# Adding two lanes of the bias network's last layer by DMA, so that TensorE closes four steps at a time instead of two

## The chip, the cores and the metric

The kernel runs on one core of one Trainium2 chip, in f32 throughout. The metric is device time in microseconds (us) of one launch, the median of several runs; lower is better.

## The reference

Two layers follow each other on x of shape (2, 512, 32, 32). The first is a deformable attention block with eight groups of 64 channels, the second a plain single-head attention over the 1024 pixels with 512 channels. Nearly all that matters here is one part of the first layer: a small network gives a bias for each pair of a pixel (1024 of them) and a sampled key (64 of them), for each of the 16 combinations of batch and group.

```python
pos  = grid_q[:, :, None, :] - grid_kv[:, None, :, :]      # 16 x 1024 x 64 x 2
bias = sign(pos) * log1p(abs(pos))
bias = relu(bias @ cpb_w1 + cpb_b1)                        # 2 -> 128
bias = relu(bias @ cpb_w2 + cpb_b2)                        # 128 -> 128, the costly one
bias = (bias @ cpb_w3 + cpb_b3)                            # 128 -> 1
sim  = q . k + bias ; attn = softmax(sim) ; out = attn . v
```

Around it lie grouped 1x1 convolutions, a 6x6 depthwise convolution that gives the keys' offsets, the sampling of the keys, an output projection, a two-layer MLP with 2048 hidden channels, and the second attention.

## The kernel before, in words

**Stages.** A head of some 42 us makes the queries and the key offsets of the first two groups. Then comes the stage of the bias network, 256 steps, up to about 1988 us. Then the projection, the MLP (each product by Strassen's seven multiplications) and the second attention, up to 2742 us. The change touches the head and the stage of the bias network.

**A step.** `NS = NG * NSL` is 16 groups times 16 steps. A step `s` handles four keys against all 1024 pixels. `st_layer1(s)` on VectorE (DVE) adds two small tables and clamps at zero: a tile `h1` of 128 channels x 4096. `st_layer2(s)` on TensorE (PE) multiplies it by `cw2`, the 128x128 weights of the second layer, in four blocks `z` of 32 output channels. Each block is eight matmuls into one PSUM tile of two banks: partition 32q + l of that tile is key q and lane l, where lane l stands for the four channels that the four blocks give at that place. ScalarE (ACT) takes each block out of PSUM with the ReLU: blocks 0 and 2 as they are into `rx`, blocks 1 and 3 scaled by their weight of the third layer into `ua` and `ub`.

**The third layer.** It is a dot product over 128 channels, and most of it is done before TensorE sees it. `st_sum(s, 0)` on DVE adds weight times `rx` to `ua`, `st_sum(s, 2)` the same for `ub`. For a scaled ReLU to keep its meaning the weights of one lane must have one sign, so the head sorts out signs: `swap` on GpSimd (POOL) exchanges channels within a lane where needed, and `sc[:, 8]` keeps the sign of each lane. Then a DMA that adds (`accum_op`), issued from POOL, adds `ub` to `ua` (line L583), for all but the last `LAST = 2` steps. `st_layer3` closes two steps at a time: four matmuls of 128x512 with `w3s`, which holds the lanes' signs, sum the 32 lanes of each key into the scores `sim` of the group in PSUM (line L604). At a group's last closing the q.k matmuls go into the same tile, and `softmax_steps` follows in the background over the next steps.

**Order.** The loop over `s` writes `st_sum(s-1, 2)`, `st_layer1(s+2)`, `st_layer2(s)`, `st_sum(s, 0)`, one piece of background work (`later`: the offsets and keys of the later groups; `softmax_steps`), and at odd `s` `st_layer3(s-3)`. A scheduler orders each engine's queue, and every engine runs its queue in order. Each wait, also for a DMA's landing, is made by the queue that holds the waiting instruction. SyncE (SP) issues `load_tables` (`fb`, once in four steps), and the loads and stores of the background work.

**Buffers.** `h1` has 3, `rx` 3, `ua` 5, `ub` 4, PSUM tiles for the blocks 3, `sim` 2.

Of the kernel before, what the change touches and what calls it, by code (L numbers as in the profile page):

```python
# [14 lines left out]
P = 128  # L15
# [7 lines left out]
LAST = 2  # L23
# [14 lines left out]
    ("w1x", 1), ("w1y", 1), ("cb2", 4), ("w3", 4), ("dww", 36),  # L38
# [10 lines left out]
def conv_seq_kernel(ctx: ExitStack, tc: tile.TileContext, x, xt, kst, cst, vec, wsm, outw, w1, w2, wl, out):  # L49
# [4 lines left out]
    kp = cp.tile([P, 384], F32, name="kp")  # L54
# [3 lines left out]
    ident = kp[:, 0:128]  # L58
# [11 lines left out]
    w3s = cp.tile([P, 60], F32, name="w3s")  # L70
    nc.gpsimd.memset(w3s, 0.0)
# [22 lines left out]
    with tc.tile_pool(name="lp", bufs=2) as lp, tc.tile_pool(name="ph", bufs=1) as ph:  # L94
# [30 lines left out]
        nc.scalar.dma_start(out=kp, in_=kst)  # L125
# [19 lines left out]
        def swap(w, of, n):  # L145
            w = w.rearrange("p (z c) -> p z c", z=4)
            t = ph.tile([P, 10, n], F32, tag="hx" if n > 1 else "swap", name=f"swap{n}")
            g, ne, a1, a3, keep, t0, t1 = t[:, 0:4], t[:, 4], t[:, 5], t[:, 6], t[:, 7], t[:, 8], t[:, 9]
            nc.gpsimd.tensor_scalar(g, w, 0.0, None, ALU.is_ge)
            for o, u, v in ((ne, g[:, 1], g[:, 3]), (a1, g[:, 0], g[:, 1])):  # L150
                nc.gpsimd.tensor_tensor(o, u, v, ALU.subtract)
                nc.gpsimd.tensor_tensor(o, o, o, ALU.mult)
            nc.gpsimd.tensor_tensor(a1, a1, ne, ALU.mult)
            nc.gpsimd.tensor_tensor(a3, ne, a1, ALU.subtract)
            nc.gpsimd.tensor_scalar(keep, ne, -1.0, 1.0, ALU.mult, ALU.add)
            for dst, src in of:
                d, v = (e.rearrange("p (z c) -> p z c", z=4) for e in (dst, src))
                nc.gpsimd.tensor_copy(d[:, 2], v[:, 2])
                nc.gpsimd.tensor_tensor(d[:, 0], v[:, 0], keep, ALU.mult)
                for z, a in ((1, a1), (3, a3)):  # L160
                    nc.gpsimd.tensor_tensor(t0, v[:, z], a, ALU.mult)
                    nc.gpsimd.tensor_tensor(d[:, 0], d[:, 0], t0, ALU.add)
                    nc.gpsimd.tensor_scalar(t1, a, -1.0, 1.0, ALU.mult, ALU.add)
                    nc.gpsimd.tensor_tensor(t1, t1, v[:, z], ALU.mult)
                    nc.gpsimd.tensor_tensor(t0, v[:, 0], a, ALU.mult)
                    nc.gpsimd.tensor_tensor(d[:, z], t0, t1, ALU.add)

        swap(kp[:, 256:384], [(cw2, kp[:, 128:256])], 32)
        w3 = vs[:, VOFF["w3"] : VOFF["w3"] + 4]
        swap(w3, [(sc[:, 0:4], w3), (sc[:, 4:8], vs[:, VOFF["cb2"] : VOFF["cb2"] + 4])], 1)  # L170
        nc.gpsimd.tensor_scalar(sc[:, 8:9], sc[:, 1:2], 0.0, 2.0, ALU.is_ge, ALU.mult)
        nc.gpsimd.tensor_scalar(sc[:, 8:9], sc[:, 8:9], 1.0, None, ALU.subtract)
        nc.gpsimd.tensor_scalar(sc[:, 0:4], sc[:, 0:4], sc[:, 8:9], None, ALU.mult)
        for z in (1, 3):
            nc.gpsimd.tensor_tensor(sc[:, 4 + z : 5 + z], sc[:, 4 + z : 5 + z], sc[:, z : z + 1], ALU.mult)
        for u in range(4):
            nc.gpsimd.tensor_copy(w3s[32 * u : 32 * u + 32, 28 + u : 29 + u], sc[32 * u : 32 * u + 32, 8:9])
# [154 lines left out]
        def sample(ci):  # L332
# [23 lines left out]
            for i, (b, k) in enumerate(G):  # L356
# [29 lines left out]
                for f in range(2):  # L386
                    r = slice(64 * f, 64 * f + 64)
                    d = kvz[r, f, :].rearrange("p (e i t) -> p e i t", e=2, t=4)
                    v, u = (
                        t[r].rearrange("p (i e t) -> p e i t", e=2, t=4)  # L390
                        for t in (ps[:, 0:J], sg[:, 4, f, i * J : (i + 1) * J])
                    )
                    for e in range(2):
                        nc.vector.scalar_tensor_tensor(
                            d[:, e], v[:, e], bns[r, k : k + 1], u[:, e], ALU.mult, ALU.add
                        )
# [103 lines left out]
        for _ in head:  # L500
            pass
        next(v)
# [55 lines left out]
        def st_layer2(s):  # L558
            h1 = h1s.pop(s)
            r = []  # L560
            for z in range(4):
                ps = zp.tile([P, 2, 512], F32, name="ps2")
                for h in range(2):
                    for q in range(4):
                        nc.tensor.matmul(  # L565
                            ps[32 * q : 32 * q + 32, h, :], cw2[:, 32 * z : 32 * z + 32],
                            h1[:, 16 * h : 16 * h + 16, q, :], start=True, stop=True,
                        )
                o = lp.tile([P, 2, 512], F32, name=("rx", "ua", "rx", "ub")[z], bufs=(3, 5, 3, 4)[z])
                if z % 2 == 0:  # L570
                    nc.scalar.activation(o, ps, AF.Relu, bias=sc[:, 4 + z : 5 + z])  # L571
                else:
                    nc.scalar.activation(o, ps, AF.Relu, bias=sc[:, 4 + z : 5 + z], scale=sc[:, z : z + 1])  # L573
                r.append(o)
                if z % 2 == 1:
                    evicted.setdefault(s, []).append(nc.cur_bb.bb.instructions[-1])
            sums[s] = r

        def st_sum(s, z):
            r = [t.rearrange("p h n -> p (h n)") for t in sums[s][z : z + 2]]  # L580
            nc.vector.scalar_tensor_tensor(r[1], r[0], sc[:, z : z + 1], r[1], ALU.mult, ALU.add)  # L581
            if z == 2 and s < NS - LAST:
                nc.gpsimd.dma_start(out=sums[s][1], in_=sums[s][3], accum_op=ALU.add)  # L583

        def st_layer3(s):
            gi, i = divmod(s // 2, NSL // 2)
# [3 lines left out]
            if i == NSL // 2 - 1:  # L590
# [8 lines left out]
            parts = (1,) if s < NS - LAST else (1, 3)  # L599
            for z in parts:  # L600
                for h in range(2):
                    for e in range(2):
                        q = 64 * h + 32 * e
                        nc.tensor.matmul(  # L604
                            sims[gi][q : q + 32, :], w3s[:, 28 - 4 * i : 60 - 4 * i], sums[s + e][z][:, h, :],
                            start=(i == 0), stop=(i == NSL // 2 - 1 and z == parts[-1]),
                        )
            for e in range(2):
                sums.pop(s + e)
# [63 lines left out]
        for s in range(NS):  # L673
            if s > 0:
                st_sum(s - 1, 2)
            if s % 4 == 0 and s // 4 + 1 < 4 * NG:
# [15 lines left out]
            if s % 2 == 1 and s >= 3:  # L692
                st_layer3(s - 3)
                if (s - 2) % NSL == NSL - 1:
                    tail = softmax_steps(s // NSL - 1)
        st_sum(NS - 1, 2)
        st_layer3(NS - 2)
# [455 lines left out]

def _layout(np, inputs):
# [7 lines left out]
    def twice(v):  # L1162
# [8 lines left out]
        "cb2": np.tile(L0["cpb_b2"].reshape(4, 32).T, (4, 1)),  # L1171
        "w3": np.tile(L0["cpb_w3"].reshape(4, 32).T, (4, 1)),
# [27 lines left out]
    def quarters(w):  # L1200
# [9 lines left out]
        "kst": np.concatenate(  # L1210
            [np.eye(P, dtype=np.float32), L0["cpb_w2"], np.broadcast_to(L0["cpb_w3"].reshape(1, P), (P, P))],
            axis=1,
        ),
# [26 lines left out]
```

## Time and profile before

| | |
|---|---|
| median of 3 runs | 2741.42 us (2740.01 to 2743.95) |
| time of the profiled execution | 2744.24 us |
| its span, first to last instruction | 2742.5 us |
| granted TensorE clock | 0.998 |
| PE busy | 2721.3 us, 99% of the span |
| DVE busy | 2248.2 us, 82% |
| ACT busy | 1686.6 us, 61% |
| POOL busy | 374.7 us, 14% |
| DMA busy in most of the stage (mean of 16 engines) | four tenths |

Busy time is the union of an engine's instructions; a group's "mean ns" is that of one record, and an f32 matmul leaves two records. Matmuls overlap in the array, so that the mean duration of one is not what it costs: the distance from one start to a later one is. Idle time before a group is put down to the engine or DMA that ended it. A DMA's time "to landing" counts from the start of its issue on the queue that issues it.

### The profile page before, as it was taken

How to read it: one execution, taken by the hardware profiler on the slowest of the kernel's cores; microseconds unless marked ns; L12 is line 12 of the kernel's file. 1: busy time of each engine (PE TensorE's matmuls, PEld its weight loads, DVE VectorE, ACT ScalarE, POOL GpSimd, SP SyncE). 2: the span in 40 equal slices, each digit the busy share in tenths (PEclk: the TensorE clock that was granted, in tenths of full speed). 3: DMA queues.
4: the chain of work that ended last, by engine and by line, in shares of the span. 5: the costliest groups of instructions: out<-in, count | busy, mean ns of one | idle time of the engine just before them, and what ended most of it. 6: DMA issues, size and time to landing. Idle time of an engine off the chain costs nothing.

```text
span 2742.5 us, 46612 instructions
## 1 busy us (share of the span) xinstructions
PE 2721.3 (99%) x20114; PEld 975.2 (36%) x20114; DVE 2248.2 (82%) x1327; ACT 1686.6 (61%) x2164; POOL 374.7 (14%) x430
## 2 busy tenths in 40 slices
PE   9999999999999999999999999999999999999999
PEld 3322323233334333333333333333334444446455
DVE  6999999998999899999999999999774574466454
ACT  4786897788878788866866776686722022124040
POOL 3111111111111111111111111111162233000000
PEclk9999999999999999999999999999999999999999
DMA  5444444444444444444444444444331011000000
GB/s 186 93 95 94 91 97 86 94 99 95 86 88 98 101 85 85 95 92 86 89 95 88 85 93 89 89 93 86 70 138 43 35 46 46 16 16 0 31 0 31
DMA packets 64685, 214.32 MB, mean 78 GB/s; under 512 B 11104, under 2 KB 13664, under 8 KB 61792
## 3 DMA queue, kind: packets, MB, share of 16 engines
q0 software_dynamic: 36864, 135.28, 26.7%
q1 hardware_dynamic: 26752, 74.98, 7.7%
q8 instruction: 159, 2.61, 0.4%
q10 hardware_dynamic: 864, 1.07, 0.1%
q14 instruction: 46, 0.38, 0.0%
HBM read 71.59 MB, written 6.55 MB: 28 GB/s over the span
## 4 chain that ended last, share of the span: by engine, by line
PE 91%; DVE 4%; issue 2%; ACT 2%; DMA 1%; SPq 0%; POOL 0%; DVEq 0%; ACTq 0%; POOLq 0%
PE ps L565 58%; PE sw L850 14%; PE sw L967 9%; PE sim L604 4%; PE sw L1065 2%; DVE h L548 2%; PE sw L796 1%; PE psg L454 1%; DVE ua L581 0%; PE sim L595 0%; DVE ub L581 0%; DMA fb<-fdr 0%; PE pkv L380 0%; DMA ua<-ub 0%; ACT rx L571 0%
## 5 line engine op out<-in xcount | busy, mean ns | idle before, releaser
L565 PE MATMUL ps<-h,cw 128*32 128x512 f32 x16384 | 1790.9, 593 | 7.1 <-ACT rx L571 4.8
L548 DVE CUSTOM_DVE_ANT_1 h<-ta,tb 128x4096 f32<-128x4096 f32 (+1 forms) x257 | 1131.7, 4404 | 88.7 <-PE ps L565 85.0
L565 PEld LDWEIGHTS ps<-h,cw 128*32 128x32 f32 x16384 | 535.4, 110 | 1224.0 <-issue 1170.2
L571 ACT ACTIVATE rx<-ps,sc 128x1024 f32<-128x1024 f32 x512 | 568.7, 1111 | 219.7 <-PE ps L565 216.3
L583 POOL DMA_DIRECT2D ua<-ub x254 | 220.5, 868 | 1697.2 <-DVE ub L581 1609.4
L573 ACT ACTIVATE ua<-ps,sc 128x1024 f32<-128x1024 f32 x256 | 308.4, 1205 | 117.1 <-PE ps L565 116.7
L573 ACT ACTIVATE ub<-ps,sc 128x1024 f32<-128x1024 f32 x256 | 307.9, 1203 | 89.3 <-PE ps L565 89.0
L581 DVE SCALAR_TENSOR_TENSOR ua<-rx,sc,ua 128x1024 f32<-128x1024 f32 x256 | 327.4, 1279 | 34.8 <-ACT ua L573 34.6
L581 DVE SCALAR_TENSOR_TENSOR ub<-rx,sc,ub 128x1024 f32<-128x1024 f32 x256 | 326.7, 1276 | 5.8 <-ACT ub L573 5.6
L850 PE MATMUL sw<-xb,w1t 128*128 128x512 f32 x448 | 193.7, 592 | 1.3 <-DVE xs L730 1.3
L850 PE MATMUL sw<-hm,w2t 128*128 128x512 f32 x448 | 193.6, 592 | 0.0
L730 DVE TENSOR_TENSOR hm<-hm,sw 128x1024 f32<-128x1024 f32 x56 | 67.6, 1219 | 112.4 <-PE sw L850 112.2
L604 PE MATMUL sim<-ua,w3s 128*32 128x512 f32 x1024 | 135.5, 594 | 0.2 <-DMA ua<-ub 0.2
L850 PEld LDWEIGHTS sw<-xb,w1t 128*128 128x128 f32 x448 | 85.0, 190 | 108.8 <-issue 105.2
L850 PEld LDWEIGHTS sw<-hm,w2t 128*128 128x128 f32 x448 | 85.1, 190 | 107.1 <-issue 106.4
L859 ACT ACTIVATE hm<-hm,vs 128x512 f32<-128x512 f32 x64 | 42.7, 714 | 129.4 <-DVE hm L730 129.4
L730 DVE TENSOR_TENSOR xs<-xs,sw 128x1024 f32<-128x1024 f32 (+1 forms) x48 | 55.5, 1170 | 75.7 <-PE sw L967 36.0
L529 ACT ACTIVATE ta<-fb,vs 128x512 f32<-128x512 f32 x64 | 88.3, 1379 | 17.5 <-DMA fb<-fdr 17.5
L967 PE MATMUL sw<-aT,vt 128*128 128x512 f32 x224 | 96.7, 593 | 0.3 <-ACT aT L1047 0.3
L884 ACT COPY hm<-sw 128x1024 f32<-128x1024 f32 x8 | 8.1, 1010 | 133.6 <-PE sw L850 133.6
L714 POOL TENSOR_TENSOR w1t<-w1t 128x512 f32<-128x512 f32 x32 | 60.4, 1909 | 111.7 <-DMA w1t<-in_w 111.1
L245 ACT ACTIVATE prod<-qa,vs 128x56 f32<-128x56 f32 (+4 forms) x180 | 64.0, 440 | 0.0
(221 smaller groups left out, 1551.4 us busy)
## 6 DMA issues: line engine op xcount, KB each, us to landing
ua<-ub POOLq DMA_DIRECT2D x254, 512.0 KB, 4.7
fb<-fdr SPq DMA_DIRECT2D x64, 512.0 KB, 5.1
w1t<-in_w SPq DMA_DIRECT2D x8, 1024.0 KB, 4.9
w2t<-in_w SPq DMA_DIRECT2D x8, 1024.0 KB, 4.8
xn<-in_x SPq DMA_DIRECT2D x8, 512.0 KB, 5.2
xnt<-in_xt SPq DMA_DIRECT2D x8, 512.0 KB, 5.7
xs<-in_x SPq DMA_DIRECT2D x16, 256.0 KB, 5.9
out<-xs SPq DMA_DIRECT2D x16, 256.0 KB, 2.1
```

What stands on the lines that cost most here:

```text
L245: nc.scalar.activation(dst, src, AF.Copy, scale=col("dww", 12 * m + t))
L529: nc.scalar.activation(ta.rearrange("p j x -> p x j"), fb[:, 0], AF.Identity, bias=col("cb1"), scale=col("w1x"))
L548: nc.vector._custom_dve(TENSOR_ADD_SAT, out=h1[:, y : y + step].rearrange("p y t x -> p (y t x)"), in0=a.unsqueeze(1).to_broadcast([P, ste ...
L565: nc.tensor.matmul(ps[32 * q : 32 * q + 32, h, :], cw2[:, 32 * z : 32 * z + 32], h1[:, 16 * h : 16 * h + 16, q, :], start=True, stop=True,)
L571: nc.scalar.activation(o, ps, AF.Relu, bias=sc[:, 4 + z : 5 + z])
L573: nc.scalar.activation(o, ps, AF.Relu, bias=sc[:, 4 + z : 5 + z], scale=sc[:, z : z + 1])
L581: nc.vector.scalar_tensor_tensor(r[1], r[0], sc[:, z : z + 1], r[1], ALU.mult, ALU.add)
L583: nc.gpsimd.dma_start(out=sums[s][1], in_=sums[s][3], accum_op=ALU.add)
L604: nc.tensor.matmul(sims[gi][q : q + 32, :], w3s[:, 28 - 4 * i : 60 - 4 * i], sums[s + e][z][:, h, :], start=(i == 0), stop=(i == NSL // 2 ...
L730: nc.vector.tensor_tensor(out, a, b_, op)
L850: nc.tensor.matmul(ps[:, m, :], w[:, a, k, m * P : (m + 1) * P], x[:, b_, k, :], start=(k == 0), stop=(k == 1),)
L967: nc.tensor.matmul(ps[:, m, :], w[:, a, k, c + m * P : c + (m + 1) * P], x[b_][:, k, :], start=(k == 0), stop=(k == nk - 1),)
```

## The change

**Tiles of eight keys by sixteen sums.** After `ub` has been added to `ua`, two more additions by DMA halve the lanes. For an even step `st_fold` adds the odd partitions of its tile to the even ones (64 partitions, accumulating, POOL). For the odd step after it `st_join` first copies that step's odd partitions over the freed odd partitions of the even step's tile (64 partitions, plain copy, SP), and then adds its even partitions to them (64 partitions, accumulating, POOL). One tile then holds eight keys with sixteen sums each. `st_layer3` closes four steps with four matmuls, and stands one step later than before: at `s % 4 == 2` for the steps s-6 to s-3. The softmax of a group starts one step later as well. The last four steps are closed without fold and join, by ten matmuls with `w3u`.

**Channels by sign.** For lanes to be added in pairs, both must have the same sign. The exchange by `swap` on POOL goes. Instead the head ranks all 128 channels by the sign of their weight (two matmuls of one column, a copy on ACT, three small instructions on POOL, six on DVE), forms a permutation matrix, and `arrange` multiplies the weights with it (one matmul of 128 columns and sixteen of two columns, two copies on ACT, seven small instructions on POOL). The constants for that come in a new load `pst` of 413 columns on ACT's queue, at the place where `kst` (384 columns) was loaded; `kst` is cut to 128 columns and follows.

**Buffers.** The five `ua` become four for even and two (`uo`) for odd steps; `ub` goes from four to three.

```diff
-LAST = 2
...
-        nc.scalar.dma_start(out=kp, in_=kst)
+        pz, pw_ = (
+            lp.tile([P, 2, 512], F32, tag="rx", name=n, bufs=3).rearrange("p h n -> p (h n)")
+            for n in ("pz", "pwork")
+        )
+        nc.scalar.dma_start(out=pz[:, 0:413], in_=pst)
+        nc.scalar.dma_start(out=ident, in_=kst)
...
-        swap(kp[:, 256:384], [(cw2, kp[:, 128:256])], 32)
...
+        nc.gpsimd.memset(one, 1.0)
+        nc.gpsimd.tensor_scalar(po_, wb[:, 0:1], 0.0, None, ALU.is_ge)
+        ps = flat("rank")
+        nc.tensor.matmul(ps[:, 0:1], tri, po_, start=True, stop=True)
+        nc.tensor.matmul(ps[:, 512:513], one, po_, start=True, stop=True)
+        nc.scalar.copy(rn, ps.rearrange("p (h n) -> p h n", h=2)[:, :, 0])
...
+        nc.vector.tensor_scalar(perm, place, pc, None, ALU.is_equal)
+
+        def arrange():
+            ps = flat("perm")
+            nc.tensor.matmul(ps[:, 0:P], w2t, perm, start=True, stop=True)
+            for z in range(4):
+                for u in range(4):
+                    nc.tensor.matmul(
+                        ps[32 * u : 32 * u + 32, 512 + 2 * z : 514 + 2 * z], perm[:, 32 * z : 32 * z + 32], wb,
+                        start=True, stop=True,
+                    )
+            nc.scalar.copy(cw2, ps[:, 0:P])
...
         for _ in head:
             pass
+        arrange()
...
-                o = lp.tile([P, 2, 512], F32, name=("rx", "ua", "rx", "ub")[z], bufs=(3, 5, 3, 4)[z])
+                name, bufs = (("rx", 3), (("ua", 4), ("uo", 2))[s % 2], ("rx", 3), ("ub", 3))[z]
+                o = lp.tile([P, 2, 512], F32, name=name, bufs=bufs)
...
-            if z == 2 and s < NS - LAST:
+            if z == 2 and s < NS - 1:
                 nc.gpsimd.dma_start(out=sums[s][1], in_=sums[s][3], accum_op=ALU.add)
 
+        def lanes(s, i):
+            return sums[s][1].rearrange("(l e) h n -> l e (h n)", e=2)[:, i]
+
+        def st_fold(s):
+            nc.gpsimd.dma_start(out=lanes(s, 0), in_=lanes(s, 1), accum_op=ALU.add)
+
+        def st_join(s):
+            nc.sync.dma_start(out=lanes(s, 1), in_=lanes(s + 1, 1))
+            nc.gpsimd.dma_start(out=lanes(s, 1), in_=lanes(s + 1, 0), accum_op=ALU.add)
...
-            parts = (1,) if s < NS - LAST else (1, 3)
...
+            w = w3f[:, 24 - 8 * i : 56 - 8 * i]
+            parts = [[(w, sums[s + 2 * e][1])] for e in range(2)]
+            if s + 4 == NS:
+                w = [w3u[:, 28 - 8 * i - 4 * o : 60 - 8 * i - 4 * o] for o in range(2)]
+                parts = [[(w[o], sums[s + 2 * e + o][1]) for o in range(2)] for e in range(2)]
+                parts[1].append((w[1], sums[s + 3][3]))
...
             if s > 0:
                 st_sum(s - 1, 2)
+            if s % 2 == 0 and 2 <= s < NS - 2:
+                st_fold(s - 2)
+            if s % 2 == 1 and 3 <= s < NS - 1:
+                st_join(s - 3)
...
-            if s % 2 == 1 and s >= 3:
-                st_layer3(s - 3)
-                if (s - 2) % NSL == NSL - 1:
+            if s % 4 == 2 and s >= 6:
+                st_layer3(s - 6)
+                if (s - 2) % NSL == 0:
                     tail = softmax_steps(s // NSL - 1)
         st_sum(NS - 1, 2)
-        st_layer3(NS - 2)
+        st_layer3(NS - 4)
```

## The prediction, made before the changed kernel ran

> **What bounds the kernel now.** I read the busy shares first, then the chain that ended last, then the costliest groups, and then one stretch of the stage in order of time.
>
> ```profile
> PE 2721.3 (99%) x20114; PEld 975.2 (36%) x20114; DVE 2248.2 (82%) x1327; ACT 1686.6 (61%) x2164; POOL 374.7 (14%) x430
> PE 91%; DVE 4%; issue 2%; ACT 2%; DMA 1%; SPq 0%; POOL 0%; DVEq 0%; ACTq 0%; POOLq 0%
> ...
> L565 PE MATMUL ps<-h,cw 128*32 128x512 f32 x16384 | 1790.9, 593 | 7.1 <-ACT rx L571 4.8
> L548 DVE CUSTOM_DVE_ANT_1 h<-ta,tb 128x4096 f32<-128x4096 f32 (+1 forms) x257 | 1131.7, 4404 | 88.7 <-PE ps L565 85.0
> ...
> L604 PE MATMUL sim<-ua,w3s 128*32 128x512 f32 x1024 | 135.5, 594 | 0.2 <-DMA ua<-ub 0.2
> ...
> ua<-ub POOLq DMA_DIRECT2D x254, 512.0 KB, 4.7
> ```
>
> PE is busy 99%, and the chain is PE for 91%. Its layer-2 groups (L565) wait 7.1 us in all, the closings (L604) 0.2 us; DVE waits 85.0 us for PE. So in the stage PE sets the pace, nearly without holes, and PE time taken out is time won until another engine or DMA catches up. What a closing costs is seen in the timeline (start, duration):
>
> ```profile
> 999.89 1.04 PE L604 MATMUL sim<-ua,w3s 128*32 128x512 f32 x8
> 1000.75 13.92 PE L565 MATMUL ps<-h,cw 128*32 128x512 f32 x128
> 1014.48 1.04 PE L604 MATMUL sim<-ua,w3s 128*32 128x512 f32 x8
> 1015.34 13.92 PE L565 MATMUL ps<-h,cw 128*32 128x512 f32 x128
> ```
>
> From closing to layer 2 it is 0.86 us for eight records; two steps take 14.59 us, 13.73 of them layer 2 (6.87 a step). Over the stage, with background work, two steps take (1988 - 42)/128 = 15.2 us.
>
> DVE is the next bound, as busy time in windows of 60 us shows (length, then PE, PEld, DVE, ACT, POOL with records):
>
> ```profile
> 400.00:460.00 60.00, 59.97 (x564) 18.32 (x560) 58.98 (x32) 51.35 (x69) 6.88 (x8) 1.00 0.40 86
> 700.00:760.00 60.00, 60.00 (x564) 18.22 (x558) 59.92 (x32) 51.37 (x67) 6.88 (x8) 1.00 0.44 89
> 1000.00:1060.00 60.00, 60.00 (x563) 18.67 (x556) 60.00 (x32) 51.20 (x68) 6.88 (x8) 1.00 0.43 89
> 1660.00:1720.00 60.00, 60.00 (x568) 18.12 (x563) 56.14 (x26) 41.18 (x37) 7.37 (x9) 1.00 0.44 89
> ```
>
> Where offsets of later groups are computed DVE is full too; from 1240 us on it has some 4 us free in 60.
>
> **What the Trainium skill says.** "DMA: Bandwidth & Descriptors", section "SWDGE vs HWDGE vs iDMA": a DMA that accumulates must come from GpSimd, and all queues share 16 engines. The trace agrees: the software queue, POOL's, holds 26.7% of them. The same page, "Two DMAs through the same engine are not ordered": a DMA that needs another's data must be held back by its issuer until that one's semaphore. No run here shows it yet; it means that POOL and SP stand still for each fold, copy and join. The same page, "Anatomy of one DMA", prices a transfer at 2.0 us + bytes/436e3, so 3.2 us for 512 KB. The trace has 4.7 for the accumulating one, and I use that.
>
> **Part by part.**
>
> 1. *Closings.* The built programs hold 516 and 262 matmuls of this kind: 254 fewer, each group of four at 0.86 us: 63.5 x 0.86 = **-54.6 us**, all on PE's path. The q.k matmuls stay.
>
> 2. *Folds and joins* (126 folds, 126 copies, 126 joins, one more addition of `ub`). Priced at nothing if they hide; what hides them is PE's layer 2. The work is a ring on POOL and SP over two steps: addition for the even step, fold (waits for its landing), addition for the odd step, copy on SP (waits for that landing), join (waits for the copy), next even addition behind it in POOL's queue. Prices: an addition lands after 4.7 us, and holds POOL for 0.86. A 64-row one isn't in the trace; POOL's hold is between half of 0.86 and 0.86, I take 0.86; landing between 2.7 and 4.7, I take 3.1 (half the data time). The copy: 2.1 us is the nearest row (stores of 256 KB), 2.6 the page's formula, 5.9 the slowest load; I take 2.5. Ring: 4.7 + 0.86 + 4.7 + 2.5 + 0.86 = **13.6 us**, between 12.0 and 17.0. Two steps after the change take 13.73 + 0.43 = 14.2 bare and 15.2 - 0.43 = 14.8 with background work. It fits by 0.6 to 1.2 us. The even addition falls 0.5 to 1 us behind DVE, which the wait for the odd sum (about 7 us after the even one) takes up.
>    - Does PE wait? Counted from an even addition, the odd one starts at 7, lands at 11.7, copy 14.2, join lands 17.3; the closing stands some 21 us after that start (6.2 us after a step's end, then four steps of 6.87). Slack 4 us; before it is 3.1 (an addition issued at 1021.37 lands 1026.0, its closing is at 1029.07).
>    - Buffers: `uo` is needed again four steps later, some 7 us after the join; `ub` after three, 8 us after its addition. Covered.
>    - Queues: SP also holds `fb` loads (they wait for ACT's `tb`) and stores of the offsets, which wait for DVE. In the built order three groups of stores and one pair of `fb` loads stand just before a copy and can hold it 4 to 5 us, about the slack. POOL's `kvz` memsets wait for PE, little. I put **+3 us** for it all (0 to 15).
>    - The 16 DMA engines: four tenths busy, plus half of POOL's share and the copies, some six tenths. No bound.
>
> 3. *DVE.* Its work is the same, so where it is full PE can't run ahead. 60 us save 8.2 x 0.2145 = 1.76 us; room is less in the windows at 160 (58.42), 400, 700, 760 (59.93), 1000 and 1060 (59.93): together 7.7 us of the saving has no room there. `h1` is built two steps ahead, which swallows some: **+4 us** (0 to 8). ACT (51 of 60) has room.
>
> 4. *Head.* The new load takes the place of one of nearly its size, whose first reader started late:
>
> ```profile
> 4.59 0.33 ACTq L125 DMA_DIRECT2D kp<-in_kst  x1
> 6.99 1.09 PE L198 MATMUL psq<-xn,ws 64*64 64x512 f32 x8 [0.39 <-ACT xn L190]
> 8.96 0.54 POOL L149 TENSOR_SCALAR swap<-kp 128x128 f32<-128x128 f32 x1 [0.83 <-DMA kp<-in_kst]
> ```
>
>    The built order has the two rank matmuls ahead of psq in PE's queue, so psq waits for this load: 9.0, plus four records at 0.115 us (16 of one column took 1.84): 9.5 instead of 6.99, **+2.5 us**. Everything behind (ACT's copies, DVE's taps, `fdr`, `fb`, `h`) shifts with it. The new instructions of ACT, POOL and DVE fit beside psq and ACT's four copies (2.36 us). `arrange` stands in PE's queue before the products of layer 1's weights: two records of 128 columns at 0.27, and 32 of two columns, between 0.033 (four L565 weight loads take 0.13) and 0.115 each: 1.6 to 4.2, taken 2.5. That is on the path, since PE worked up to the first step:
>
> ```profile
> 38.14 3.56 PE psg L454 x8
> 41.70 0.04 DVEq L548
> 41.73 1.57 DVE h L548
> ...
> 43.35 6.22 PE ps L565 x56
> ```
>
>    PE then ends at 41.70 + 5.0 = 46.7, goes through the first half step (0.86) and starts the second at 47.6 instead of 43.35: **+4.2 us** (+1 to +9; the upper end if PE's clock drops in its gap of 2.4 us before the rank matmuls, as it did after a gap of 2.54 us at 512 us, where the windows show 0.66 of the clock from 514 to 519). Taking `swap` off POOL gains nothing, as nobody waited for it.
>
> 5. *End of the stage.* Last closing: ten matmuls after the last step instead of twelve; the last addition now goes by DMA for the step before the last one too, issued some 3 us into the last step, landing before it ends. 0.
>
> Sum: -54.6 + 3 + 4 + 4.2 = -43.4 on the span of 2742.5. The profiled execution took 2744.24, 2.8 above the median of 2741.42; the forecast is against that median: **2698 us**.
>
> **Rivals.**
>
> - *The ring sets the pace, slower.* If an addition lands after 5.6 us (one in ten of before takes 5.8 or more) and the copy after 2.7, the ring is 5.6 + 0.86 + 5.6 + 2.7 + 0.86 = 15.6 us, and 126 x (15.6 - 15.2) + 4 = +54: 2795 us. It decides above 15.2 us a ring; between 14.8 and 15.2 it eats the gain. For it: each part waits for the last one's landing, and DMA load rises by half. Against it: an undisturbed addition lands after 4.5, and within the ring hardly two transfers overlap.
> - *DVE bounds the first 1200 us.* Then the gain is only that of the last 750 us: 12.5 windows x 1.76 = 22, less 4 for the head: 2723 us. For it: the windows at 700 and 1000. Against it: they are short, and the windows between have 2 to 8 us free.
> - *Cancelled:* ring near 15.1: 2737 to 2747.
>
> The matmuls are gone in the built program, so that the change doesn't do what it says is excluded for PE.
>
> **Numbers.** 0.2% (5.5 us) is about what a measurement can tell from no change. Forecast 0.64, own range 2685 to 2715; DVE or a ring just under 15 us 0.12 (2715 to 2736); cancelled 0.05; slower 0.19, from 2747 up to 2850. The range goes from 2684 to 2765, which leaves out some 0.15 of slow cases and little below. Faster 0.76, same 0.05, slower 0.19.
>
> **What the profile after would show.** Right: closings of x524 records, at 0.86 us a group of four once in four steps; four steps at 28.3 us; PE busy 98% or more; joins landing 2 us or more before their closing; the first layer-2 matmul 4 to 5 us later. Wrong: PE idle before closings with a DMA as releaser; POOL waiting for landings all the time with DVE waiting in turn; additions landing at 5.5 us or more at the median; PE idle on `h` for tens of us.

## The result, and the profile after

The changed kernel takes **2883.4 us** (median of 4 runs, 2880.09 to 2886.71), the kernel before 2741.7 us in the same session. The ratio is 1.0516, with a 95% interval from 1.0498 to 1.0535: slower by 142 us, where 2698 us was forecast. The profiled execution took 2886.71 us, its span is 2884.9 us.

The page of the changed kernel: first busy times and the chain, then groups (busy, mean ns of one | idle before, and what ended it), then DMA issues (KB each, us to landing).

```profile
PE 2745.2 (95%) x19644; PEld 1107.1 (38%) x19644; DVE 2255.4 (78%) x1333; ACT 1682.4 (58%) x2167; POOL 590.4 (20%) x629
PE 58%; DMA 20%; issue 12%; ACT 4%; POOL 3%; DVE 1%; SPq 0%; POOLq 0%; ACTq 0%; DVEq 0%
...
L619 POOL DMA_DIRECT2D ua<-uo x126 | 106.6, 846 | 947.6 <-DMA ua<-uo 929.9
L615 POOL DMA_DIRECT2D ua<-ua x126 | 106.7, 847 | 655.7 <-DMA ua<-ub 634.8
L648 PE MATMUL sim<-ua,w3f 128*32 128x512 f32 x504 | 127.0, 672 | 104.8 <-DMA ua<-uo 104.7
L607 POOL DMA_DIRECT2D ua<-ub x128 | 155.7, 1216 | 16.6 <-DVE ub L605 13.7
...
ua<-ub POOLq DMA_DIRECT2D x128, 512.0 KB, 5.7
uo<-ub POOLq DMA_DIRECT2D x127, 512.0 KB, 5.5
...
ua<-ua POOLq DMA_DIRECT2D x126, 256.0 KB, 3.2
ua<-uo SPq DMA_DIRECT2D x126, 256.0 KB, 2.3
ua<-uo POOLq DMA_DIRECT2D x126, 256.0 KB, 3.3
```

The closings (L648) have shrunk as planned, from 1024 records to 504. But a DMA now releases them after 104.8 us of idle time, where it was 0.2 us, and DMAs make up 20% of the chain, which was PE for 91%. The telling rows are POOL's. This is its row on the page of the kernel before:

```profile
L583 POOL DMA_DIRECT2D ua<-ub x254 | 220.5, 868 | 1697.2 <-DVE ub L581 1609.4
```

There POOL stood for 1609.4 us waiting for DVE: it was early. Now its additions (L607, even steps) wait 13.7 us for DVE, while its joins (L619) wait 929.9 us and its folds (L615) 634.8 us for landings. POOL is late, and what it waits for are DMAs that it or SP issued a moment earlier. The additions land 5.7 and 5.5 us after their issue; before it was 4.7.

The waits ahead of closings (104.8 us) are less than the loss (142 us). Part of the rest is TensorE's granted clock: its mean is 0.981 in this run and 0.998 in the kernel before, which is some 49 us of 2885. The trace has 25 stretches at half the clock, mostly of 3.4 or 6.8 us, 24 of them at a wait of PE of 1.9 us or more. Whether they add to the loss, or fill time in which PE would have waited for the ring anyway, isn't shown.

One ring in the changed kernel's timeline (start, duration; in brackets the idle time before and what ended it):

```profile
1505.15 0.85 POOL L619 DMA_DIRECT2D ua<-uo  x1 [7.80 <-DMA ua<-uo]
1505.68 1.23 POOL L607 DMA_DIRECT2D ua<-ub  x1
...
1508.48 0.81 PE L648 MATMUL sim<-ua,w3f 128*32 128x512 f32 x3 [3.01 <-DMA ua<-uo]
...
1511.43 0.85 POOL L615 DMA_DIRECT2D ua<-ua  x1 [4.51 <-DMA ua<-ub]
1511.97 1.24 POOL L607 DMA_DIRECT2D uo<-ub  x1
...
1517.57 0.47 SPq L618 DMA_DIRECT2D ua<-uo  x1
...
1520.33 0.85 POOL L619 DMA_DIRECT2D ua<-uo  x1 [7.13 <-DMA ua<-uo]
1520.87 1.23 POOL L607 DMA_DIRECT2D ua<-ub  x1
```

Join, even addition right behind it, a wait for its landing, fold, odd addition right behind that, its landing, the copy on SP, its landing, the next join: 15.18 us from join to join here, 16.34 on the mean of 125 rings. PE closes at 1508.48, the moment the join of 1505.15 lands, after 3.01 us of idle time. Of 63 closings 55 start, or go on after their first matmuls, within 0.6 us of the landing of their second join.

### The profile page after: what moved, and what is told of

Read it like the earlier page. It is cut to its first block, busy times and chain, and to the rows that moved or that the text cites. A ratio compares the mean times of both kernels' runs of the same rounds, so it can differ in the third digit from the quotient of the medians.

```text
span 2884.9 us, 47006 instructions
## 1 busy us (share of the span) xinstructions
PE 2745.2 (95%) x19644; PEld 1107.1 (38%) x19644; DVE 2255.4 (78%) x1333; ACT 1682.4 (58%) x2167; POOL 590.4 (20%) x629
## 3 DMA queue, kind: packets, MB, share of 16 engines
q1 hardware_dynamic: 36832, 108.02, 10.3%
## 4 chain that ended last, share of the span: by engine, by line
PE 58%; DMA 20%; issue 12%; ACT 4%; POOL 3%; DVE 1%; SPq 0%; POOLq 0%; ACTq 0%; DVEq 0%
PE ps L588 30%; PE sw L898 13%; DMA ua<-uo 10%; DMA uo<-ub 9%; PE sw L1015 8%; PE sim L648 2%; POOL ua L607 2%; PE sw L1113 2%; PE psg L476 1%; PE sw L844 1%; POOL ua L615 1%; ACT rx L595 1%; POOL ua L619 1%; ACT prod L267 1%; ACT ub L597 0%
## 5 line engine op out<-in xcount | busy, mean ns | idle before, releaser
L588 PE MATMUL ps<-h,cw 128*32 128x512 f32 x16384 | 1863.3, 602 | 20.1 <-ACT rx L595 14.5
L588 PEld LDWEIGHTS ps<-h,cw 128*32 128x32 f32 x16384 | 680.1, 111 | 1136.6 <-issue 1012.0
L619 POOL DMA_DIRECT2D ua<-uo x126 | 106.6, 846 | 947.6 <-DMA ua<-uo 929.9
L605 DVE SCALAR_TENSOR_TENSOR uo<-rx,sc,uo 128x1024 f32<-128x1024 f32 x128 | 164.0, 1281 | 172.5 <-ACT uo L597 172.0
L615 POOL DMA_DIRECT2D ua<-ua x126 | 106.7, 847 | 655.7 <-DMA ua<-ub 634.8
L648 PE MATMUL sim<-ua,w3f 128*32 128x512 f32 x504 | 127.0, 672 | 104.8 <-DMA ua<-uo 104.7
L597 ACT ACTIVATE uo<-ps,sc 128x1024 f32<-128x1024 f32 x128 | 154.1, 1204 | 56.4 <-PE ps L588 54.5
L597 ACT ACTIVATE ua<-ps,sc 128x1024 f32<-128x1024 f32 x128 | 154.0, 1203 | 51.2 <-PE ps L588 50.6
L605 DVE SCALAR_TENSOR_TENSOR ua<-rx,sc,ua 128x1024 f32<-128x1024 f32 x128 | 163.8, 1279 | 17.2 <-ACT ua L597 17.0
L607 POOL DMA_DIRECT2D ua<-ub x128 | 155.7, 1216 | 16.6 <-DVE ub L605 13.7
L607 POOL DMA_DIRECT2D uo<-ub x127 | 155.3, 1223 | 8.2 <-DVE ub L605 8.2
```

The costliest lines, as they stand in the source:

```text
L588: nc.tensor.matmul(ps[32 * q : 32 * q + 32, h, :], cw2[:, 32 * z : 32 * z + 32], h1[:, 16 * h : 16 * h + 16, q, :], start=True, stop=True,)
L615: nc.gpsimd.dma_start(out=lanes(s, 0), in_=lanes(s, 1), accum_op=ALU.add)
L619: nc.gpsimd.dma_start(out=lanes(s, 1), in_=lanes(s + 1, 0), accum_op=ALU.add)
L648: nc.tensor.matmul(sims[gi][q : q + 32, :], w_, t[:, h, :], start=(i == 0), stop=(i == NSL // 4 - 1 and m == len(parts[e]) - 1),)
```

## The experiments

The theory after this reading: **the pace of a serial ring on POOL's queue**. The loop writes the fold behind the odd addition and the join behind the next even addition. In the order that the scheduler built each stands ahead of that addition, so that three landings in a row (even addition, odd addition, copy) are waited for between one join and the next. The rivals: the load of the 16 DMA engines (six tenths where it was four), VectorE, the head, and a moment rather than a pace, namely that only the last join lands too late for its closing.

### Only the order of POOL's queue

```diff
                 nc.gpsimd.dma_start(out=sums[s][1], in_=sums[s][3], accum_op=ALU.add)
+                added[s] = nc.cur_bb.bb.instructions[-1]
...
-                st_fold(s - 2)
+                with tc.issue_after(added[s - 1]):
+                    st_fold(s - 2)
...
-                st_join(s - 3)
+                with tc.issue_after(added[s - 1]):
+                    st_join(s - 3)
```

`issue_after` fixes the place in the queue and waits for nothing.

> All the work of the changed kernel is kept; only the order of POOL's queue is fixed as it is written in the loop: the fold stands behind the odd step's addition, the join behind the next even step's addition (in the changed kernel the scheduler had put each ahead of that addition). No wait is added or taken away. Theory (serial ring on POOL's queue: in the changed kernel addition, fold, addition, copy and join each stand for the landing before them, 16.3 us a ring where PE needs 14.8 for two steps): an addition is now issued while the other DMAs are under way, POOL's waits for landings (929.9 and 634.8 us) fall below a third, PE is bound by its own work again, and the time is 2741.7 - 54.6 (closings) + 2.8 (head, as measured) + 0 to 15 = 2690 to 2705 us. Rival, load: the 16 DMA engines at six tenths make every transfer slow, whatever the order; then additions and joins land as late as now and the time stays at 2860 to 2890. Rival, DVE: VectorE is full in the first 1200 us and the gain of the closings stays out there: 2715 to 2730.

Measured: 2786.5 us, ratio 1.0165 (1.0151 to 1.0179). The order alone gives back 97 us, with no DMA, wait or instruction removed, so load can't explain that part. But none of the three numbers is met: the kernel stays 45 us slower than the kernel before and 80 us slower than the next one. The page of this run (the join's waits, and how the fold lands):

```profile
L620 POOL DMA_DIRECT2D ua<-uo x126 | 109.3, 868 | 470.7 <-DMA ua<-uo 443.2
...
ua<-ua POOLq DMA_DIRECT2D x126, 256.0 KB, 6.8
```

The join waits 443.2 us where it was 929.9. The fold, which now stands right behind the odd addition, lands 6.8 us after its issue instead of 3.2, and the copy has to wait for it, so that the join lands 15.9 us after the odd addition's issue (median; 12.1 in the changed kernel).

### No folds, copies or joins

```diff
-                st_fold(s - 2)
+                pass
...
-                st_join(s - 3)
+                pass
```

> The changed kernel without its folds, copies and joins (378 DMAs); the closings of four steps, the additions, the new head and the buffers stay. Left out of the computation: half of the lanes and half of the keys don't reach their scores. Theory (all of the loss comes from these DMAs): 2741.7 - 54.6 + 2.8 = 2690, with up to 8 us for DVE: 2690 to 2698. Rival (the order of the closings, the smaller pools of ua, uo and ub, or DVE hold PE): 2715 or more, and whatever stands above 2690 here can't be put down to the ring.

Measured: 2706.6 us, ratio 0.9871 (0.9858 to 0.9885). The 378 DMAs thus cost 2883.4 - 2706.6 = 177 us, and all of the loss lies in them. The kernel without them is 9 us above the upper end of the expectation; the run with less work on VectorE below shows most of what that is. Its stage is also the measure of PE's own pace: layer 2 runs from 45.4 to 1949.2 us, that is 14.87 us for two steps.

### Each copy twice

```diff
             nc.sync.dma_start(out=lanes(s, 1), in_=lanes(s + 1, 1))
+            nc.sync.dma_start(out=lanes(s, 1), in_=lanes(s + 1, 1))
```

> The changed kernel with POOL's order written out as the scheduler had it (join, even addition, fold, odd addition), and each copy made twice, one behind the other, on SP. The second copy waits for the first, 2.3 us to land and 0.3 to 0.6 of hand-over, and moves 256 KB more. Theory (serial ring): 126 x 2.6 to 2.9 = +330 to +365 us on 2883: 3210 to 3250. Rival, load of the DMA engines: the copies are 108 us of the engines' busy time in 2885 (10.3% incl. the other loads on that queue); twice of the copies' part adds about 3% of load and 5 to 30 us: 2890 to 2915.

Measured: 3203.7 us, ratio 1.1686 (1.1670 to 1.1702). The ring grew from 16.34 to 18.91 us, and 126 x 2.57 = 324 us against 320 measured. One element of the ring was made 2.6 us longer, and the mean ring took it in full, so that there is no slack to hide it. The lower end of the expectation was 3210; the result lies 6 us below that; that the load alone does it (2890 to 2915) is out. In this run POOL's order is written out and in the changed kernel it is the scheduler's; in a later pair that differs in this alone it is worth 8 us (2861.3 and 2853.4).

### The new head alone

Against the kernel before; the stage, its buffers and closings are unchanged:

```diff
-        nc.scalar.dma_start(out=kp, in_=kst)
+        nc.scalar.dma_start(out=pz[:, 0:413], in_=pst)
+        nc.scalar.dma_start(out=ident, in_=kst)
...
-        swap(kp[:, 256:384], [(cw2, kp[:, 128:256])], 32)
...
+        nc.tensor.matmul(ps[:, 0:1], tri, po_, start=True, stop=True)
+        nc.tensor.matmul(ps[:, 512:513], one, po_, start=True, stop=True)
...
+        arrange()
```

> The kernel before with the new head alone (constants pst, rank, arrange instead of swap); the stage with its closings of two steps, its buffers and its order are those of before. Theory: only the later start of the stage counts, +2.8 us as the traces of before and after have it at the second half step (43.35 to 46.1): 2744.5 us, that is 1.001. The step of the prediction had +4.2 (1 to 9). Rival: the new order of the channels changes what the steps cost (other weights in the blocks), or DVE's slack absorbs the shift: 2741 or less, or above 2751.

Measured: 2746.7 us, ratio 1.0018 (1.0011 to 1.0024), so +4.8 us, between 3.0 and 6.6. The first layer-2 matmul starts at 46.8 us in this run and at 41.6 in the kernel before, and the last one 4.9 us later: the head's delay is paid in full. The 2.8 us of the expectation came from the trace of the changed kernel, whose first layer-2 matmul stands at 45.2 us.

### Only the join put back

```diff
                 st_fold(s - 2)
...
-                st_join(s - 3)
+                with tc.issue_after(added[s - 1]):
+                    st_join(s - 3)
```

> All the work of the changed kernel; only the join is fixed behind the next even step's addition, while the fold keeps the place ahead of the odd addition that the scheduler gave it. POOL's order is then: even addition, join, fold, odd addition. Theory: in the run with both pinned the fold stands right behind the odd addition and lands only 6.8 us after its issue, the copy waits for it, and the joins land 14.8 us after the odd addition, about when the closing stands (some 14): half the loss is latency. With the fold ahead, the copy waits for the odd addition alone: 5.5 + 0.14 + 2.3 + 0.53 + 3.3 = 11.8 us, and POOL's queue has 7.4 us a step for a hold of 0.86, a join's wait of about 1 and a fold's wait of 5. No loss is left but that of the kernel without these DMAs (2706.6): 2706 to 2722. Rival, load: additions and joins meet more traffic than before in any order, and the time stays near the run with both pinned: 2780 to 2800.

Measured: 2758.2 us, ratio 1.0064 (1.0051 to 1.0076). A miss for both. It is better than with both put back, so the fold is better left ahead of the odd addition, as the theory had it; but the joins don't land 11.8 us after the issue of the odd addition, they take 14.3 at the median (15.9 with both put back). The page of this run shows most of the reason:

```profile
ua<-ub POOLq DMA_DIRECT2D x128, 512.0 KB, 4.6
uo<-ub POOLq DMA_DIRECT2D x127, 512.0 KB, 6.2
...
ua<-uo POOLq DMA_DIRECT2D x126, 256.0 KB, 4.1
```

The odd addition stands right behind the fold and lands after 6.2 us, the join right behind the even addition and lands after 4.1. The even addition, which follows nothing, lands after 4.6. The expectation had used 5.5 and 3.3. The copies add the rest: 2.3 us at the median, as expected, but 3.1 on the mean. Of 63 closings 40 still start, or go on, within 0.6 us of the landing of their join.

### Order as written, and the closing one step later

On top of both DMAs fixed behind their additions, as in the first run:

```diff
-            if s % 4 == 2 and s >= 6:
-                st_layer3(s - 6)
+            if s % 4 == 3 and s >= 7:
+                st_layer3(s - 7)
```

> As the run with both DMAs pinned (2786.5 us), and the closing of four steps stands one step later (step s closes s-7 to s-4), which gives every join 7 us more to land; order and waits of POOL's and SP's queues are the same. Theory (what is left there is latency: joins that land about when their closing stands): 2706 to 2725. Rival (throughput of the queues or of the DMA engines): the ring has the same pace, PE is held by other means, `uo` or `ub` that come free late, and the time stays at 2770 to 2790.

Measured: **2706.6 us**, ratio 0.9873 (0.9860 to 0.9887): the time of the kernel without folds, copies and joins, with all 378 of them in it, and faster than both kernels. Its timeline, POOL and the closing:

```profile
1500.26 0.90 POOL L607 DMA_DIRECT2D ua<-ub  x1 [5.95 <-DVE ub L605]
...
1506.03 0.85 POOL L620 DMA_DIRECT2D ua<-uo  x1 [4.87 <-DMA ua<-uo]
1507.13 0.90 POOL L607 DMA_DIRECT2D uo<-ub  x1 [0.26 <-DVE ub L605]
1507.71 1.20 POOL L616 DMA_DIRECT2D ua<-ua  x1
1514.00 0.90 POOL L607 DMA_DIRECT2D ua<-ub  x1 [5.09 <-DVE ub L605]
...
1515.55 1.04 PE L649 MATMUL sim<-ua,w3f 128*32 128x512 f32 x8
1516.41 4.05 PE L588 MATMUL ps<-h,cw 128*32 128x512 f32 x36
1516.63 0.85 POOL L620 DMA_DIRECT2D ua<-uo  x1 [1.73 <-DMA ua<-uo]
```

Each addition is again released by DVE, 6.87 us apart. POOL waits a few us for a landing (L620), but inside time in which it would have waited for DVE. The closing of 1515.55 has no idle time before it, and layer 2 goes on 0.86 us later; no closing of this run starts within 2.3 us of its join's landing, the median is 6.2. The joins still land 15.6 us after the odd addition's issue (16.2 for the second joins of a closing, which it waits for). The closings now stand 23.0 us after that issue; at the old place they would stand about one step, 7.4 us, earlier, so at 15.6, at the landing or just ahead of it. That is what was left in the run with the order alone.

The load rival has fallen with this run: the same bytes in less time (DMA six to seven tenths busy in nearly all of the stage), and the time of the kernel without them.

### The closing one step later, without the order

POOL's queue is written out as the scheduler had it (join, even addition, fold, odd addition), and then:

```diff
-            if s % 4 == 2 and s >= 6:
-                st_layer3(s - 6)
+            if s % 4 == 3 and s >= 7:
+                st_layer3(s - 7)
```

> The changed kernel with POOL's order written out as the scheduler had it (join, even addition, fold, odd addition), and the closing of four steps one step later; single copies. In the changed kernel 55 of 63 closings start within 0.6 us of the landing of their second join, so that either the pace of the ring or the moment of its last landing can be what holds PE. Theory, pace: the sum of what stands in series on POOL, even undisturbed, is 0.54 + 5.45 + 0.29 + 0.54 + 5.45 + 0.14 + 2.25 + 0.53 = 15.2 us, 16.3 on the mean, against some 14.6 for two steps of the kernel without these DMAs; a later closing changes nothing of that, PE is then held by the buffers that come free late, and the time is 2706.6 + 126 x (0.6 to 1.7) = 2780 to 2890. Rival, moment: only the landing of the second join comes too late, one step more takes that away, and the time is that of the run with both pinned and the late closing: 2706 to 2715.

Measured: 2861.3 us, ratio 1.0434 (1.0417 to 1.0452). The same edit that gives 80 us where the order is right gives 22 here (30 in the one-line version below): most of the loss is a pace, not a moment. The ring takes 16.13 us, and 2706.6 + 126 x (16.13 - 14.87) = 2865. The wait has only moved, to where the theory had put it. Waits in this run (in total, times, longest), and PE's row for layer 2 from its page:

```profile
POOL ua L630 <- DMA ua<-uo: 957.5, 125, 9.9
POOL ua L624 <- DMA ua<-ub: 596.7, 124, 7.1
ACT uo L603 <- DMA ua<-uo: 247.6, 70, 5.4
...
L594 PE MATMUL ps<-h,cw 128*32 128x512 f32 x16384 | 1812.1, 597 | 105.4 <-ACT uo L603 57.2
```

The closings wait 1.2 us in all, where it was 104.8. ACT now waits 247.6 us for a free `uo`, which the join has not read yet, and PE's layer-2 groups stand idle for 105.4 us, 57.2 of them until ACT has read a block into `uo`.

The one-line version of it, the changed kernel with nothing but the later closing and the order left to the scheduler:

> The changed kernel with nothing but its closing one step later; POOL's order is left to the scheduler, which builds the same one as in the changed kernel for most of the stage (even addition, fold, odd addition, join), with a join ahead of the odd addition in places. As for the run with the order written out: by the pace of the ring 2780 to 2890, by the moment of the landing 2706 to 2715.

Measured: 2853.4 us, ratio 1.0405 (1.0389 to 1.0420). The same answer.

### Less work on VectorE

On top of the kernel without folds, copies and joins:

```diff
-            st_sum(s, 0)
+            if s % 2 == 0:
+                st_sum(s, 0)
```

> As the kernel without folds, copies and joins (2706.6 us), and without the first of the two sums on VectorE in odd steps: 128 instructions of 1.28 us, 164 us of its 2252. Left out of the computation, beside half of the lanes: block 0 of the odd steps. Theory (what stands there above 2692, that is 2741.9 - 54.6 + 4.8, is VectorE being full in the first 1200 us): 2680 to 2692, since the kernel before loses some 12 us to VectorE as well. Rival (the order of the closings or the smaller pools hold PE): 2702 to 2707.

Measured: 2696.2 us, ratio 0.9834 (0.9820 to 0.9847), 10.4 us less. Windows of the kernel without folds, copies and joins, where the offsets of later groups are computed (length, then busy PE, PEld, DVE, ACT, POOL with records, clock, DMA share, GB/s):

```profile
160.00:260.00 100.00, 100.00 (x940) 30.56 (x936) 99.81 (x62) 78.40 (x97) 11.34 (x14) 1.00 0.42 83
460.00:560.00 100.00, 98.03 (x936) 29.93 (x932) 99.94 (x61) 74.81 (x80) 11.70 (x14) 1.00 0.45 95
760.00:860.00 100.00, 99.04 (x944) 30.84 (x944) 100.00 (x60) 81.78 (x116) 12.20 (x14) 1.00 0.46 96
1060.00:1160.00 100.00, 99.21 (x940) 32.18 (x936) 99.97 (x61) 84.92 (x131) 12.19 (x14) 1.00 0.42 88
```

DVE is full in all four and PE has holes in three. With the lighter DVE its busy time there is 93.84, 92.73, 92.10 and 90.37. PE's holes (starts of neighbouring records over 0.6 us apart, less the usual distance) sum to 13.7 us over the stage of the kernel before, 30.7 in the kernel without folds, copies and joins, and 19.5 here. The 17 us more are about the 14.5 us that stand above 2741.9 - 54.6 + 4.8 = 2692.1, and the lighter VectorE takes 11 of them away. That PE is held by the order of the closings or by the smaller pools alone (2702 to 2707) is out. How much of the 10.4 us belongs to the change is not shown: the kernel before has holes of 13.7 us too, and it was not run with the lighter VectorE, which might shorten it as well. The run is 4 us above the range expected; what holds these 4 us was not tried.

### Why the additions land late

The largest error of the ring is the landing of the additions, and four single runs look at it outside the ring: the kernel without folds, copies and joins, with one more DMA of POOL right ahead of each addition. They have one execution each, with 255 landings in it.

Plain and small, in the second of the two with 256 columns in place of 8:

```diff
+                nc.gpsimd.dma_start(out=ahead[0:64, 0, 0:8], in_=sums[s][3][0:64, 0, 0:8])
                 nc.gpsimd.dma_start(out=sums[s][1], in_=sums[s][3], accum_op=ALU.add)
```

> The kernel without folds, copies and joins, with a plain transfer of 64 rows of 32 bytes (2 KB in all, to a tile that nobody reads) issued on POOL right ahead of each addition of ub. In the changed kernel an addition that is issued within 0.9 us of another DMA of POOL lands after 5.6 us at the median and hardly under 5.45, against 4.58 in the kernel without these DMAs. Theory, issue (POOL or its queue takes longer for the second of two DMAs, whatever they carry): the additions land after 5.4 us or more here too. Rival, data (the 256 KB of the join share the 16 engines with the addition): they land after 4.6 to 4.8. The time tells little: 2706 to 2715 in both cases, as the closings have slack.

> As before, with 64 rows of 1 KB (64 KB in all) ahead of each addition, as much as the place in SBUF allows; the join has 64 rows of 4 KB. Theory, issue: the additions land as late as behind the 2 KB transfer, 5.4 us or more. Rival, data: 0.1 to 0.3 us later than behind the 2 KB transfer, for a quarter of the join's bytes.

Adding, with the size of a join, and in the second of the two without `accum_op`:

```diff
+                nc.gpsimd.dma_start(out=sums[s][2][0:64], in_=sums[s][3][0:64], accum_op=ALU.add)
                 nc.gpsimd.dma_start(out=sums[s][1], in_=sums[s][3], accum_op=ALU.add)
```

> The kernel without folds, copies and joins, with an adding transfer of 64 rows of 4 KB from ub to the first half of the tile rx of the same step (nobody reads that again) right ahead of each addition: the join's kind and size, with no wait for anything that VectorE has not just finished. Small and plain transfers ahead left the additions at 4.66 and 4.72 us. Theory, data (the second transfer stands behind the first one's 256 KB on the engines): the additions land after 5.4 to 5.6 us, as in the changed kernel. Rival (their lateness there comes from other traffic of the ring, not from the transfer just ahead): they stay at 4.7 to 4.9.

> The same with a plain transfer of 64 rows of 4 KB ahead of each addition instead of an adding one. Theory, bytes alone: the additions land as late as behind the adding transfer, 5.4 us or more. Theory, adding: an adding transfer takes the engines longer than a plain one, and the additions land after 4.8 to 5.1 here.

| DMA ahead of each addition | addition lands (median) | its record on POOL | time of the one run |
|---|---|---|---|
| none | 4.58 us | 0.87 us | 2706.6 (median of 4) |
| plain, 2 KB | 4.66 us | 0.96 us | 2707.1 |
| plain, 64 KB | 4.72 us | 0.96 us | 2710.3 |
| plain, 256 KB | 5.30 us | 0.96 us | 2712.7 |
| adding, 256 KB | 7.03 us | 1.22 us | 2725.8 |
| join or fold (the changed kernel) | 5.60 us | 1.22 us | 2883.4 |

The page of the run with the adding transfer:

```profile
ua<-ub POOLq DMA_DIRECT2D x128, 512.0 KB, 6.9
rx<-ub POOLq DMA_DIRECT2D x255, 256.0 KB, 4.6
uo<-ub POOLq DMA_DIRECT2D x127, 512.0 KB, 7.4
```

That the mere issue ahead does it has fallen: 2 KB cost 0.08 us. 64 KB add 0.06 more, less than the 0.1 expected. The two large ones met no number: 7.03 us is above 5.4 to 5.6, and 5.30 lies between the two theories, so that both the bytes and the adding count. POOL's queue on the pages of these two runs, plain, then adding (packets, MB, share of the 16 engines):

```profile
q0 software_dynamic: 57408, 202.67, 38.5%
q0 software_dynamic: 57408, 202.67, 49.7%
```

The same packets and bytes take more engine time when they are added. Without a DMA ahead the share is 26.3%, so that the adding transfers take nearly twice what the plain ones do.

The Trainium skill, "DMA: Bandwidth & Descriptors", section "Two DMAs through the same engine are not ordered", says that within one queue of one DMA engine descriptors start in order, though they are pipelined. All of POOL's DMAs are on one queue of the profile (q0), so that an addition should start behind the transfer issued before it. The packets of the traces agree. An addition with nothing ahead of it moves its first data 1.44 us after its issue. Where it follows another DMA, the data of that one end 2.37 us after its issue behind a fold or join of the changed kernel, 2.15 behind the plain transfer of 256 KB and 3.73 behind the adding one (medians). An estimate that adds the difference to 1.44 us to the 4.58 us gives landings after 5.5, 5.3 and 6.9 us; measured are 5.60, 5.30 and 7.03. So an addition lands late by the time that the data ahead of it on the queue still take.

Why the adding transfer of this run takes longer than a fold or join (it lands after 4.6 us, they after 3.2 to 3.3) is in the packets too: a packet of 4 KB takes 0.67 us on rows 0 to 63 and 0.34 on every second row (medians). The mean number of packets under way is 15 in both, so that it isn't fewer engines. Why a packet takes longer was not tried.

## Why the prediction was wrong

The account: 2741.9 - 54.6 (closings, counted) + 4.8 (head, measured) + 14.5 (the rest up to the kernel without folds, copies and joins; VectorE for up to 10 of it) + 176.8 (folds, copies, joins, measured) = 2883.4.

1. **Closings: not contradicted.** 504 records are left in the trace of the 524 that were counted (some records are missing from it). A group of four still takes 0.86 us (1515.55 to 1516.41 in the run with the order and the late closing). The kernel without the new DMAs comes within 14.5 us of this step's gain.
2. **Folds and joins, +3 us: this step failed.** Its order of the ring was the one on the trace, and its condition was the right one, that the ring fits into PE's two steps. Its sum was too small (each "landing to" row is the hand-over from a landing to the issue that waits for it; the measured terms are means over the changed kernel's rings; in a few of them the even addition stands ahead of the join, which lowers the first one):

| term | predicted | measured (mean) |
|---|---|---|
| join to even addition | 0.86 | 0.32 |
| even addition lands | 4.7 | 6.14 |
| landing to fold | - | 0.31 |
| fold to odd addition | 0.86 | 0.60 |
| odd addition lands | 4.7 | 5.85 |
| landing to copy | - | 0.14 |
| copy lands | 2.5 | 2.44 |
| landing to join | - | 0.55 |
| sum | 13.6 | 16.34 |

   The landings of the additions are 2.6 us of the 2.7. Their 4.7 us came from a kernel in which nothing of POOL's stood ahead of them; in the ring each follows a join or a fold. It was a median as well, where a sum over many rings needs the mean, which is 5.0 in the kernel before: 0.6 of the 2.6 us. The hand-overs (1.0 us) were not in the sum, the holds were too large by 0.8: the record of a fold or join on POOL lasts 0.85 us, but the next one starts after 0.54. The copy's 2.5 us was right, though the formula among its reasons isn't made for it: the Trainium skill ("DMA: Bandwidth & Descriptors", section "Anatomy of one DMA") gives that fit for DMAs issued from GpSimd, and SP issues the copy. The ring's range had 17.0 as its upper end, so the value was inside it and the choice was not; the term's own 0 to 15 us allowed no ring much above 15.2. The judgement "within the ring hardly two transfers overlap" was the error: in 110 of 125 rings both pairs of them follow each other within 0.6 us, by the order that the prediction itself had written down. With 16.34, the formula of the first rival gives 2741.4 + 126 x (16.34 - 15.2) + 4 = 2889.
   - "Slack 4 us" for the closing was not checked against a late odd addition: the join lands 12.1 us after that addition's issue in the changed kernel and 15.9 us in the one with the order put right, not 10.3.
   - "Buffers: covered" holds only while the ring keeps pace; with the later closing and the ring left, `uo` is what ACT waits for.
   - "The 16 DMA engines: no bound" was right, as the run with the order and the later closing shows.
3. **VectorE, +4 us: probably too small.** Of the 14.5 us that are left, the lighter VectorE takes away 10, some of which the kernel before may lose as well. The loss of room was read from windows in which DVE had just some us free; with PE faster, four windows of 100 us are full to 99.8% and more.
4. **Head, +4.2 us: right**, 4.8 measured (3.0 to 6.6). `psq` starts at 9.51 us in the changed kernel, as worked out; the first layer-2 matmul comes 3.6 us later there and 5.1 us later in the run of the new head alone.
5. **End of the stage, 0:** the rest of the kernel after the last closing takes 751.3 us in place of 752.5.

Of the rivals, the first ("the ring sets the pace, slower", chance 0.19) is what happened, further out than its 2795 us and than the 2850 us that the prediction gave as the end of the slow cases. Of the signs named as wrong, three came: PE idle ahead of closings with a DMA as releaser, POOL waiting for landings all the time, additions at 5.5 us or more at the median.

## What to carry to other kernels

When dependent DMAs share one engine's queue, write down the queue's built order and add up everything that stands in series from one issue to the same issue a period later, with hand-overs; take means, not medians; and a landing time is only good for an issue with the same transfer ahead of it. Put an independent issue ahead of the instruction that waits for a landing, and give the last landing a step more before its reader: here the order and one step of delay turned 142 us lost into 35 won (2706.6 against 2741.7 us), without an instruction less. Either alone did not: 2786.5 and 2853.4 us.

## What the hardware showed that was not expected

- A 512 KB addition lands after 4.58 us alone, 5.30 right behind a plain and 7.03 right behind an adding transfer of 256 KB on the same queue, and 4.66 behind one of 2 KB. Of these two large transfers, with the same rows and bytes, a packet of 4 KB took 0.67 us where it was added and 0.33 where it was copied.
- An adding DMA's record on POOL lasts 0.85 us with 64 rows and 0.87 with 128, a plain one's with 64 rows 0.54. Right behind an adding one it lasts 1.22 us, but that record starts 0.54 us behind the other: the two together last 1.77 us, hardly more than 0.85 + 0.87.
- Packets of the adding transfer took 0.67 us on rows 0 to 63, and those of folds and joins on every second row 0.34, with 15 under way on the mean in both.
- From a landing to the next issue it takes 0.29 us where POOL waits for its own DMA, 0.53 where it waits for SP's, and 0.12 where SP waits for POOL's (medians, changed kernel).
